# A graph layer on one core: layer 0's keys by nodes, its norms a round further ahead, two steps on GpSimd, six zero scatters, and the last group's transposes inside the context

## Chip, core, metric

One core of one Trainium2 chip runs the whole kernel. The metric is the device time of one execution in microseconds (us), as a median over runs. The engines are written as in the profile: PE (TensorE matmul), PEld (its weight loads), DVE (VectorE), ACT (ScalarE), POOL (GpSimd), SP (SyncE, which only issues DMAs here).

## What is computed

The reference takes 6250 nodes of 256 features and 106250 edges of 64 features:

```python
xn = _layernorm(x)
x = x + gnn(xn, edges, u) + mix(xn)          # mix: four layers, below
x = x + ffn(_layernorm(x))                   # one of 32 experts for each node

# one layer of mix
h = _layernorm(x, ln1_g[i], ln1_b[i])
q = softmax(split(h @ Wq) * scale, axis=-1)  # over the 32 features of a head
k = softmax(split(h @ Wk) * scale, axis=-2)  # over all 6250 nodes
v = split(h @ Wv)
context = einsum('bhnd,bhne->bhde', k, v)
x = x + einsum('bhnd,bhde->bhne', q, context) @ Wo + bo
x = x + gelu(layernorm2(x) @ W1 + b1) @ W2 + b2
```

The gnn term sums the edges' features by source node. The softmax of `k` runs over the nodes, so its maximum and sum go over all groups of nodes before the context is complete.

## The kernel before

The nodes lie in 13 groups: twelve of 4 tiles of 128 nodes, and a last one (g = 12, `NG - 1`) of 106 nodes. `X` keeps all nodes in SBUF. Every engine runs its instructions in the order in which the code issues them; that order is written out by hand, and buffers come from pools that are used in turn. PSUM has six banks for matmuls (`mm`) and two for the edges' sums (`seg`). A float32 matmul leaves two records in the trace, so 8 matmuls in the code are `x16` in the views.

The part that the change is about mostly is layer 0's first half: it makes q, k and the context for all groups, before the first feed-forward block (`ff_in`, L258). Its loop runs over g = 0 to 11. A round g of the loop is, in the code before:

- `keys_t(g-1)` (L685, copies L687): transposes the exponentials of k of the group before, which lie by features (128 features by 512 nodes), to nodes by features, 8 transposes;
- `norms_b(g+1)` (L346 to L359): reciprocals and products for the double norm (the input's norm and the layer's own), the scaling of `X` (L353, four on DVE), ACT's square root (L351) and ACT's scaled copy to `z` (L359);
- `norms_a(g+2)` (L337, L338, L339): mean and variance of the tiles on DVE, square root on ACT;
- `keys(0, g, then=rest)`: k by features, 4 matmuls of 128x512 (L534), the maximum over the nodes (L535), the running maximum and ACT's exponential from PSUM with its sum (L554); between them `rest`, that is `queries_t(g-1)` (L698, copies L701) and `queries` twice (matmuls L575, maximum L584, difference L585, exponential L587);
- `queries_norm` twice (sum L594, reciprocal L595, product L596, all on DVE);
- `context(g-1)`: 8 matmuls (L715) and the running update (L721);
- `norm1_t(0, g+1)`: 8 transposes of `z` (L148) and ACT's scaled copies to `hT` (L152).

Rounds 1, 3, 5 and 7 also carry a little work for the edges on DVE: casts of the source numbers (L384, L808), and `edge_match` and `edge_split` (L431, L448, L450).

Layers 1 to 3 make their keys in another way, by nodes: `keys_n` (8 matmuls L609, two copies to SBUF L612, two maxima L616 and L617), `keys_max` (2 transposes L625, reduction L627), `keys_less` (2 transposes L645, two differences L648), `keys_exp` (exponentials in SBUF) and `context_n` (8 matmuls L667 of 257 columns, where a column of ones makes the sum of k). The feed-forward matmuls fill most of those layers. At the end of each of them the last full group and the group of 106 nodes take the old way, with `keys`, `context` and `norm1_t`.

The edges go through POOL: 831 scatters (L483) that add rows to four tables in HBM. Each waits until the scatter four before it has landed. Near the end POOL also scatters the nodes to the experts' table `xtab` (L1104) and the results to the output (L1201). Until its first edge scatter POOL has only memsets, iotas and one select to do.

Of the kernel before, what the change touches and what calls it, by code (L numbers as in the profile page):

```python
# [63 lines left out]
def graph_layer_kernel(ctx, tc, x, src, srct, edge, cols, rows, rwt, gw1, gw2, wq, wk, wv, wo, w1, w2, xw, out):  # L64
# [41 lines left out]
    def group(g):  # L106

        i0 = 4 * g
        n = min(4, NT - i0)
        r = min(P, N - i0 * P)  # L110
        return i0, n, r, i0 * P, min(512, N - i0 * P)
# [49 lines left out]
    with ExitStack() as body:  # L161
# [124 lines left out]
        with ExitStack() as mix:  # L286
# [44 lines left out]
            def norms_a(g):  # L331
                i0, n, r, t0, cnt = group(g)
                st = small.tile([P, 4, 6], F32, name="st")
                mv = small.tile([P, 4, 2], F32, name="mv")
                sd = small.tile([P, 4], F32, name="sd")
                for j in range(n):
                    nc.vector.bn_stats(out=st[:r, j, :], in_=X[:r, i0 + j, :])  # L337
                    nc.vector.bn_aggr(out=mv[:r, j, :], in_=st[:r, j, :])  # L338
                nc.scalar.activation(sd[:r, :n], mv[:r, :n, 1], AF.Sqrt, bias=eps[:r], scale=1.0)  # L339
                LN[g] = mv, sd  # L340

            def norms_b(g):
                i0, n, r, t0, cnt = group(g)
                mv, sd = LN.pop(g)
                rs = small.tile([P, 4], F32, name="rs")
                nc.vector.reciprocal(rs[:r, :n], sd[:r, :n])  # L346

                v1 = small.tile([P, 4], F32, name="v1")
                nc.vector.tensor_tensor(out=v1[:r, :n], in0=mv[:r, :n, 1], in1=rs[:r, :n], op=ALU.mult)
                nc.vector.tensor_tensor(out=v1[:r, :n], in0=v1[:r, :n], in1=rs[:r, :n], op=ALU.mult)  # L350
                nc.scalar.activation(v1[:r, :n], v1[:r, :n], AF.Sqrt, bias=eps[:r], scale=1.0)  # L351
                for j in range(n):
                    nc.vector.tensor_scalar(out=X[:r, i0 + j, :], in0=X[:r, i0 + j, :], scalar1=mv[:r, j, 0:1],  # L353
                                            scalar2=rs[:r, j:j + 1], op0=ALU.subtract, op1=ALU.mult)
                rs1 = small.tile([P, 4], F32, name="rs1")
                nc.vector.reciprocal(rs1[:r, :n], v1[:r, :n])
                Z1[g] = z = z1(g)
                for j in range(n):
                    nc.scalar.activation(z[:r, j, :], X[:r, i0 + j, :], AF.Copy, scale=rs1[:r, j:j + 1])  # L359


            per_row = ep.tile([P, 5], F32, name="per_row", bufs=1)
            expo, wgt, twice, dump = (per_row[:, i:i + 1] for i in range(4))
            nc.gpsimd.iota(expo, pattern=[[0, 1]], base=63, channel_multiplier=-1, allow_small_or_imprecise_dtypes=True)
            nc.scalar.activation(wgt, expo, AF.Exp, scale=float(np.log(3.0)))
# [6 lines left out]
            half = qT[:, 1, N - 2 * ET:N - ET].bitcast(I16)[:, :ET]  # L372
            nc.sync.dma_start(out=wide, in_=srct.rearrange("o (p t) -> (o p) t", p=P))
            near_row = near.rearrange("(o p) t -> o (p t)", o=1)
            dumpi = per_row[:, 4:].bitcast(I32)
            nc.gpsimd.iota(dumpi, pattern=[[0, 1]], base=TDUMP, channel_multiplier=1)
            ebuf = [ep.tile([P, CB * EB, DE + 2], F32, name=f"edge{i}", bufs=1) for i in range(4)]
            for t in ebuf:
# [13 lines left out]
            def clear_tabs():  # L392
                for t in tabs:
                    tv = t.rearrange("(q p r) c -> q p (r c)", q=TQ, p=P)
                    for q in range(TQ):
                        nc.sync.dma_start(out=tv[q], in_=zero)

            def clear(e):
                nc.sync.dma_start(out=xtab[e * XCAP:e * XCAP + XCLEAR, :].rearrange("(p r) c -> p r c", p=P),
                                  in_=zero[:, :XROW].unsqueeze(1).to_broadcast([P, XCLEAR // P, XROW]))  # L400

            EDGE, ALL, EQ, SUM, PART = {}, {}, {}, {}, {}
            steps = {"load": 0, "match": 0, "split": 0, "sum": 0, "add": 0}
# [115 lines left out]
            def norm1_t(l, g):  # L519
                i0, n, r, t0, cnt = group(g)  # L520

                HT1[g] = ap.tile([P, 2, 512], F32, name="hT1") if g + 1 < NG else ffp.tile([P, 2, 512], F32, name="hT2")
                transposed(HT1[g], [Z1[g][:, j, :] for j in range(n)], n, r, cnt, C_G1 + 2 * l, C_B1 + 2 * l)
# [63 lines left out]
                nc.scalar.activation(q[:r, :mh], q[:r, :mh], AF.Exp, scale=QK_SCALE)  # L587
                QS[g, which] = q, mh

            def queries_norm(g, which):  # L590
                q, mh = QS[g, which]
                r = group(g)[2]
                sm = small.tile([P, 2 * HEADS], F32, name="sm")
                nc.vector.tensor_reduce(out=sm[:r, :mh], in_=q[:r, :mh], axis=AX.X, op=ALU.add)  # L594
                nc.vector.reciprocal(sm[:r, :mh], sm[:r, :mh])  # L595
                nc.vector.tensor_tensor(out=q[:r, :mh], in0=q[:r, :mh],  # L596
                                        in1=sm[:r, :mh].unsqueeze(2).to_broadcast([r, mh, DH]), op=ALU.mult)


            def keys_n(l, g):  # L600
                h, w = HT1[g], WQ[l]
                kn = []
                both = [bank(), bank()]

                for j in range(2):
                    for k in range(2):
                        for i, ps in enumerate(both):
                            c = (2 * i + j) * P
                            nc.tensor.matmul(ps[:, j * D:(j + 1) * D], h[:, k, c:c + P], w[:, k, D:2 * D], start=(k == 0), stop=(k == 1))  # L609
                for ps in both:  # L610
                    t = ap.tile([P, 512], F32, name="ek", bufs=2)
                    nc.scalar.copy(t, ps)  # L612
                    kn.append(t)

                top = ap.tile([P, 512], F32, name="kt", bufs=2)
                nc.vector.tensor_tensor(out=top, in0=kn[0], in1=kn[1], op=ALU.max)  # L616
                nc.vector.tensor_tensor(out=top[:, :D], in0=top[:, :D], in1=top[:, D:], op=ALU.max)  # L617
                KN[g] = kn, top
# [85 lines left out]
                keys_t(g)  # L704
                queries_t(g)

            def context(g, blocks=(0, 1)):

                i0, n, r, t0, cnt = group(g)
                kt, alpha = KT[g]  # L710
                z = Z1[g]
                ps = bank().rearrange("p (b c) -> p b c", b=2)
                for b in blocks:
                    for j in range(n):
                        nc.tensor.matmul(ps[:, b, :], kt[b][:r, j * P:(j + 1) * P], z[:r, j, :], start=(j == 0), stop=(j == n - 1))  # L715
                if g == 0:
                    ctxt["C"] = ap.tile([P, 2, D], F32, name="C")
                    nc.vector.tensor_copy(ctxt["C"], ps)
                else:
                    for b in blocks:  # L720
                        nc.vector.scalar_tensor_tensor(out=ctxt["C"][:, b], in0=ctxt["C"][:, b], scalar=alpha[:, b:b + 1],  # L721
                                                       in1=ps[:, b], op0=ALU.mult, op1=ALU.add)
# [50 lines left out]


            norms_a(0)
            norms_b(0)
            norm1_t(0, 0)
            norms_a(1)
            norms_a(2)
            norms_b(1)  # L780
            clear_tabs()
            load_wo(0)
            load_bo(0)
# [2 lines left out]
            for g in range(NG - 1):  # L786
                if g == 0:
                    keep_warm(6)
                elif g > 1:
                    keys_t(g - 1)  # L790
                if g:
                    norms_b(g + 1)
                if g and g + 2 < NG:
                    norms_a(g + 2)

                def rest():
                    if g:
                        queries_t(g - 1)
                    queries(0, g, 0)
                    queries(0, g, 1)  # L800

                keys(0, g, then=rest)
                for i in range(2):
                    queries_norm(g, i)
                if g:
                    context(g - 1)
                if g == 3:
                    nc.vector.tensor_copy(half, wide)  # L808
                    nc.sync.dma_start(out=near, in_=half)
                    edge_load()  # L810
                    edge_load()
                elif g == 5:
                    edge_match()
                    edge_split()
                    edge_load()
                elif g == 7:
                    edge_match()
                    edge_split()
                norm1_t(0, g + 1)
                if g == 0:  # L820
                    keys_t(0)
                elif g == 1:
                    edge_tables()
            keys_t(NG - 2)

            def last_steps(l):

# [1 line left out]
                queries_t(g, (0,), between=lambda: keys_t(g + 1))  # L829
                context_last(l, (lambda: (queries_norm(g + 1, 0), queries_t(g, (1,))), lambda: queries_t(g + 1)))  # L830

            keys(0, NG - 1, then=lambda: queries(0, NG - 1, 0))
            context(NG - 2)
            last_steps(0)


            for l in range(DEPTH - 1):
# [66 lines left out]
                norm1(g + 1)  # L904
                queries_norm(g, 1)
                context(g, (0,))
                norm1_t(n, g + 1)
                context(g, (1,))
                keys(n, g + 1, then=lambda: queries(n, g + 1, 0))
                if n + 1 == DEPTH:  # L910
                    while steps["add"] < NEB:
# [607 lines left out]
```

## Time and profile before

| | |
|---|---|
| median of 3 runs | 2731.92 us (2731.6 to 2733.16) |
| the profiled execution | 2705.55 us, its span 2703.8 us |
| TensorE clock granted | 0.997 |
| PE busy | 2663.4 us, 99% |
| DVE busy | 1751.4 us, 65% |
| ACT busy | 1146.2 us, 42% |
| POOL busy | 1475.7 us, 55% |
| layer 0's first half | from the start to 193.3 us, where the first L258 begins |
| POOL's first edge scatter | 201.56 us |

The profiled execution was 26.4 us shorter than the median of the runs. A span starts at the first instruction and ends at the last. Line numbers are those of the kernel before; in the changed kernel the same code stands some lines further down. The views give the start of a group of instructions, its length, and in brackets the idle time of its engine just before it with what ended it.

### The profile page before, as it was taken

What the parts mean: (1) busy time and instruction counts of PE and PEld (TensorE: products, weight loads), DVE (VectorE), ACT (ScalarE), POOL (GpSimd) and SP (SyncE); (2) the same over time, 40 slices, a digit from 0 to 9 for tenths busy, and PEclk for the clock granted to TensorE, in tenths of its full rate; (3) what the DMA queues carried; (4) which work ended last, traced back from release to release, by engine and by line L of the source; (5) the groups of instructions that cost most, each with busy time, mean ns of one, the idle gap of its engine ahead of it and who ended that gap; (6) DMA issues with size and microseconds to landing.
All of it is one profiled execution on the core that took longest, in us unless ns stands there. A gap on an engine that the chain in (4) does not pass through costs nothing.

```text
span 2703.8 us, 38523 instructions
## 1 busy us (share of the span) xinstructions
PE 2663.4 (99%) x13639; PEld 1954.9 (72%) x13639; DVE 1751.4 (65%) x4692; ACT 1146.2 (42%) x1999; POOL 1475.7 (55%) x1117
## 2 busy tenths in 40 slices
PE   9999999999999999999999999999999999999997
PEld 6777777777777777777767777777776676677675
DVE  8976766767568667676677766666645455454474
ACT  7764443534445444343544444435422322332333
POOL 0006777777777787887867878778300100100166
PEclk9999999999999999999999999999999999999998
DMA  8006555555665556555645555544411111111362
GB/s 261 16 11 90 64 80 65 83 63 68 85 100 70 78 61 85 64 74 73 97 75 80 65 81 65 66 48 46 92 24 32 32 32 32 32 27 31 111 226 77
DMA packets 371471, 193.58 MB, mean 72 GB/s; under 512 B 265770, under 2 KB 363790, under 8 KB 371272
## 3 DMA queue, kind: packets, MB, share of 16 engines
q1 hardware_dynamic: 245416, 150.44, 22.8%
q0 software_dynamic: 125856, 40.61, 20.3%
q8 instruction: 110, 1.80, 0.3%
q14 instruction: 89, 0.73, 0.1%
HBM read 108.78 MB, written 85.70 MB: 72 GB/s over the span
## 4 chain that ended last, share of the span: by engine, by line
PE 89%; DVE 3%; ACT 2%; DMA 2%; POOL 2%; SPq 1%; issue 1%; POOLq 0%; ACTq 0%; DVEq 0%
PE mm L258 25%; PE mm L278 25%; PE mm L197 6%; PE mm L575 5%; PE mm L609 5%; PE mm L667 4%; PE mm L1006 3%; PE mm L148 3%; PE mm L1047 3%; POOL out_x L1201 1%; PE mm L715 1%; PE mm L698 1%; ACT hT L152 1%; DMA tab<-zero 1%; PE mm L1011 1%; PE mm L534 1%
## 5 line engine op out<-in xcount | busy, mean ns | idle before, releaser
L483 POOL DMA_INDIRECT tab<-s,row x831 | 1335.9, 1608 | 584.1 <-issue 227.2
L258 PE MATMUL mm<-hT,w 128*128 128x512 f32 (+1 forms) x1664 | 705.9, 572 | 0.6 <-ACT hT L152 0.4
L278 PE MATMUL mm<-w,hid 128*128 128x256 f32 x3120 | 690.6, 380 | 0.0
L278 PEld LDWEIGHTS mm<-w,hid 128*128 128x128 f32 x3120 | 587.7, 190 | 78.7
L258 PEld LDWEIGHTS mm<-hT,w 128*128 128x128 f32 x1664 | 294.7, 190 | 298.1 <-issue 285.0
L262 ACT ACTIVATE hid<-mm,col 128x512 f32<-128x512 f32 (+1 forms) x416 | 266.1, 662 | 288.0 <-PE mm L258 287.3
L1104 POOL DMA_INDIRECT xtab<-rows,to x49 | 48.1, 983 | 572.6 <-DVE to L1102 473.0
L134 ACT ACTIVATE sd<-mv,eps 128x2 f32<-128x2 f32 (+2 forms) x161 | 47.6, 296 | 692.5 <-DVE mv L133 692.3
L280 DVE TENSOR_TENSOR X<-mm,X 128x512 f32<-128x512 f32 (+1 forms) x99 | 67.6, 683 | 284.0 <-PE mm L278 284.0
L152 ACT ACTIVATE hT<-mm,col 128x512 f32<-128x512 f32 (+1 forms) x208 | 145.2, 751 | 95.4 <-PE mm L148 95.4
L575 PE MATMUL mm<-wqkv,hT 128*128 128x256 f32 (+1 forms) x784 | 177.7, 379 | 0.0
L197 PE MATMUL mm<-M,qT 128*128 128x256 f32 x720 | 163.4, 379 | 0.0
L135 DVE RECIPROCAL rs<-sd 128x2 f32<-128x2 f32 (+2 forms) x161 | 27.4, 170 | 209.3 <-ACT sd L134 209.3
L575 PEld LDWEIGHTS mm<-wqkv,hT 128*128 128x128 f32 (+1 forms) x784 | 147.3, 190 | 19.9 <-issue 0.5
L197 PEld LDWEIGHTS mm<-M,qT 128*128 128x128 f32 x720 | 133.4, 190 | 16.6
L431 DVE TENSOR_TENSOR eq<-all,srcf 128x512 bf16<-128x512 int16 x208 | 142.5, 685 | 0.1
L199 DVE TENSOR_TENSOR X<-mm,X 128x512 f32<-128x512 f32 (+1 forms) x92 | 62.2, 676 | 119.2 <-PE mm L197 119.2
L132 DVE BATCH_NORM_STATS2 st<-X 128x6 f32<-128x256 f32 (+1 forms) x327 | 132.6, 406 | 2.7
L609 PE MATMUL mm<-wqkv,hT 128*128 128x256 f32 x528 | 122.8, 386 | 2.3
L140 DVE TENSOR_SCALAR z<-X,mv,rs 128x256 f32<-128x256 f32 (+1 forms) x327 | 121.6, 424 | 4.8
L148 PE MATMUL mm<-ident,z 128*128 128x128 f32 x882 | 118.8, 274 | 3.7 <-DVE z L140 2.8
L667 PE MATMUL mm<-z,ek 128*128 128x257 f32 x528 | 120.2, 380 | 0.0
(288 smaller groups left out, 4021.4 us busy)
## 6 DMA issues: line engine op xcount, KB each, us to landing
xtab<-zero SPq DMA_DIRECT2D x32, 1036.0 KB
edge<-in_edge SPq DMA_DIRECT2D x207, 128.0 KB
all<-near SPq DMA_DIRECT2D x207, 128.0 KB
tab<-s,row POOLq DMA_INDIRECT x831
w<-in_w SPq DMA_DIRECT2D x8, 1024.0 KB
xg<-xtab SPq DMA_DIRECT2D x26, 259.0 KB
tab<-zero SPq DMA_DIRECT2D x40, 162.5 KB
tb<-tab SPq DMA_DIRECT2D x48, 130.0 KB
```

What stands on the lines that cost most here:

```text
L132: nc.vector.bn_stats(out=st[:r, j, :], in_=source(j))
L148: nc.tensor.transpose(ps[:, j * P:j * P + r], z[j][:r, k * P:(k + 1) * P], ident[:r, :r])
L152: nc.scalar.activation(hT[:, k, :cnt], ps[:, :cnt], AF.Identity, bias=col[:, bcol + k:bcol + k + 1], scale=col[:, gcol + k:gcol + k + 1])
L197: nc.tensor.matmul(ps[:r, j, :], qT[:, k, c0:c0 + r], M[:, k, :], start=(k == 0), stop=(k == 1))
L258: nc.tensor.matmul(part[i], w[:, k, b * P:(b + 1) * P], h[:, k, :cnt], start=(k == 0), stop=(k == 1))
L262: nc.scalar.activation(hid[:, :cnt], part[i], AF.Gelu, bias=col[:, c:c + 1], scale=1.0)
L278: nc.tensor.matmul(ps[:r, j, :], hid[b][:, c0:c0 + r], w[:, b, :], start=(b == 0), stop=(b == NHB - 1))
L431: nc.vector.tensor_tensor(out=eq[:, :m], in0=ALL.pop(b)[:, :m], in1=srcf[:, t0:t0 + m].unsqueeze(2).to_broadcast([P, m, P]), op=ALU.is_equal)
L483: nc.gpsimd.indirect_dma_start(out=tabs[i], out_offset=bass.IndirectOffsetOnAxis(ap=row[:, i:i + 1], axis=0), in_=s[:, i, :DE + 1], in_off ...
L575: nc.tensor.matmul(ps[:r, j * D:(j + 1) * D], h[:, k, (j0 + j) * P:(j0 + j) * P + r], w[:, k, :D], start=(k == 0), stop=(k == 1))
L609: nc.tensor.matmul(ps[:, j * D:(j + 1) * D], h[:, k, c:c + P], w[:, k, D:2 * D], start=(k == 0), stop=(k == 1))
L667: nc.tensor.matmul(ps[:, :D + 1], kn[j // 2][:, c:c + P], z[:, j, :], start=(j == 0), stop=(j == 3))
```

## The change

In layer 0's first half the keys of groups 0 to 11 are made by nodes, as in the later layers. The norms are split into five steps (`norms_a`, `norms_a_root`, `norms_b`, `norms_b_root`, `norms_z`) and run a round earlier: `norms_a` for g+3, `norms_b` for g+2, `norms_z` for g+1. The square roots of a round stand side by side on ACT. From g = 2 on, the scaling of `X` is POOL's; so is the last product of `queries_norm` in this loop. `norm1_t(g+1)` moves up to stand before `keys_less`. Six indirect scatters of zeros to unused rows of `xtab` come before the first edge scatter; they write the same rows, and each waits for the one before it. The copies of k take buffers of `hid`. In layers 1 to 3, the last group's transposes move from before the second block of `context(g, (1,))` into its middle.

```diff
+            def norms_a_root(g):
+                i0, n, r, t0, cnt = group(g)
+                mv = LN[g]
+                sd = small.tile([P, 4], F32, name="sd")
                 nc.scalar.activation(sd[:r, :n], mv[:r, :n, 1], AF.Sqrt, bias=eps[:r], scale=1.0)
                 LN[g] = mv, sd
...
-                v1 = small.tile([P, 4], F32, name="v1")
+                LN[g] = v1 = small.tile([P, 4], F32, name="v1")
                 nc.vector.tensor_tensor(out=v1[:r, :n], in0=mv[:r, :n, 1], in1=rs[:r, :n], op=ALU.mult)
                 nc.vector.tensor_tensor(out=v1[:r, :n], in0=v1[:r, :n], in1=rs[:r, :n], op=ALU.mult)
+
+                scale = nc.vector if g < 2 else nc.gpsimd
+                for j in range(n):
+                    scale.tensor_scalar(out=X[:r, i0 + j, :], in0=X[:r, i0 + j, :], scalar1=mv[:r, j, 0:1],
+                                        scalar2=rs[:r, j:j + 1], op0=ALU.subtract, op1=ALU.mult)
+
+            def norms_b_root(g):
+                i0, n, r, t0, cnt = group(g)
+                v1 = LN[g]
                 nc.scalar.activation(v1[:r, :n], v1[:r, :n], AF.Sqrt, bias=eps[:r], scale=1.0)
-                for j in range(n):
-                    nc.vector.tensor_scalar(out=X[:r, i0 + j, :], in0=X[:r, i0 + j, :], scalar1=mv[:r, j, 0:1],
-                                            scalar2=rs[:r, j:j + 1], op0=ALU.subtract, op1=ALU.mult)
+
+            def norms_z(g):
+                i0, n, r, t0, cnt = group(g)
+                v1 = LN.pop(g)
                 rs1 = small.tile([P, 4], F32, name="rs1")
                 nc.vector.reciprocal(rs1[:r, :n], v1[:r, :n])
                 Z1[g] = z = z1(g)
...
+            nowhere = per_row[:, 5:].bitcast(I32)
+            nc.gpsimd.iota(nowhere, pattern=[[0, 1]], base=NX * XCAP, channel_multiplier=1)
+
+            def even_out():
+
+                for _ in range(6):
+                    nc.gpsimd.indirect_dma_start(out=xtab, out_offset=bass.IndirectOffsetOnAxis(ap=nowhere, axis=0),
+                                                 in_=zero[:, :XROW], in_offset=None)
...
-            def queries_norm(g, which):
+            def queries_norm(g, which, by=nc.vector):
...
-                nc.vector.tensor_tensor(out=q[:r, :mh], in0=q[:r, :mh],
+                by.tensor_tensor(out=q[:r, :mh], in0=q[:r, :mh],
                                         in1=sm[:r, :mh].unsqueeze(2).to_broadcast([r, mh, DH]), op=ALU.mult)
...
-                    t = ap.tile([P, 512], F32, name="ek", bufs=2)
+
+                    t = ap.tile([P, 512], F32, name="ek", bufs=2) if l else ffp.tile([P, 512], F32, name="hid", bufs=NHB)
                     nc.scalar.copy(t, ps)
...
-            def context(g, blocks=(0, 1)):
+            def context(g, blocks=(0, 1), between=None):
...
                     for j in range(n):
+                        if between is not None and 2 * j == n:
+                            between()
                         nc.tensor.matmul(ps[:, b, :], kt[b][:r, j * P:(j + 1) * P], z[:r, j, :], start=(j == 0), stop=(j == n - 1))
...
             norms_a(0)
+            norms_a_root(0)
             norms_b(0)
+            norms_b_root(0)
+            norms_z(0)
             norm1_t(0, 0)
             norms_a(1)
+            norms_a_root(1)
             norms_a(2)
+            norms_a_root(2)
             norms_b(1)
+            norms_b_root(1)
+            norms_b(2)
+            norms_z(1)
+            norms_b_root(2)
             clear_tabs()
...
             for g in range(NG - 1):
                 if g == 0:
                     keep_warm(6)
-                elif g > 1:
-                    keys_t(g - 1)
+                else:
+                    keys_exp(g - 1)
+                    norms_z(g + 1)
+                    if g + 2 < NG:
+                        norms_b(g + 2)
+                if g + 3 < NG:
+                    norms_a(g + 3)
+                keys_n(0, g)
                 if g:
-                    norms_b(g + 1)
-                if g and g + 2 < NG:
-                    norms_a(g + 2)
-
-                def rest():
-                    if g:
-                        queries_t(g - 1)
-                    queries(0, g, 0)
-                    queries(0, g, 1)
-
-                keys(0, g, then=rest)
+                    queries_t(g - 1)
+                    if g + 2 < NG:
+                        norms_b_root(g + 2)
+                if g + 3 < NG:
+                    norms_a_root(g + 3)
+                queries(0, g, 0)
+                keys_max(g)
+                queries(0, g, 1)
+                norm1_t(0, g + 1)
+                keys_less(g)
+                if g:
+                    context_n(g - 1)
                 for i in range(2):
-                    queries_norm(g, i)
-                if g:
-                    context(g - 1)
+                    queries_norm(g, i, by=nc.gpsimd)
...
-                norm1_t(0, g + 1)
-                if g == 0:
-                    keys_t(0)
-                elif g == 1:
+                if g == 1:
                     edge_tables()
-            keys_t(NG - 2)
+            keys_exp(NG - 2)
+            even_out()
...
-            keys(0, NG - 1, then=lambda: queries(0, NG - 1, 0))
-            context(NG - 2)
+            keys(0, NG - 1, then=lambda: (queries(0, NG - 1, 0), context_n(NG - 2)))
             last_steps(0)
...
-                norm1_t(n, g + 1)
-                context(g, (1,))
+                context(g, (1,), between=lambda: norm1_t(n, g + 1))
```

More of the change, by code (lines that the diff above doesn't have):

```diff
@@ L334, in norms_a @@
                 mv = small.tile([P, 4, 2], F32, name="mv")
-                sd = small.tile([P, 4], F32, name="sd")
                 for j in range(n):
@@ L338, in norms_a @@
                     nc.vector.bn_aggr(out=mv[:r, j, :], in_=st[:r, j, :])
+                LN[g] = mv
+            def norms_a_root(g):
+                i0, n, r, t0, cnt = group(g)
+                mv = LN[g]
+                sd = small.tile([P, 4], F32, name="sd")
                 nc.scalar.activation(sd[:r, :n], mv[:r, :n, 1], AF.Sqrt, bias=eps[:r], scale=1.0)
@@ L359, in norms_b @@
                     nc.scalar.activation(z[:r, j, :], X[:r, i0 + j, :], AF.Copy, scale=rs1[:r, j:j + 1])
-            per_row = ep.tile([P, 5], F32, name="per_row", bufs=1)
+            per_row = ep.tile([P, 6], F32, name="per_row", bufs=1)
             expo, wgt, twice, dump = (per_row[:, i:i + 1] for i in range(4))
@@ L374, in graph_layer_kernel @@
             near_row = near.rearrange("(o p) t -> o (p t)", o=1)
-            dumpi = per_row[:, 4:].bitcast(I32)
+            dumpi = per_row[:, 4:5].bitcast(I32)
             nc.gpsimd.iota(dumpi, pattern=[[0, 1]], base=TDUMP, channel_multiplier=1)
```

## The prediction

> **What bounds the kernel now.** I read the page's engine totals first, then the stretches of layer 0's first half, then the chain of waits through them.
>
> ```profile
> span 2703.8 us, 38523 instructions
> PE 2663.4 (99%) x13639; PEld 1954.9 (72%) x13639; DVE 1751.4 (65%) x4692; ACT 1146.2 (42%) x1999; POOL 1475.7 (55%) x1117
> POOL 0006777777777787887867878778300100100166
> ```
>
> PE is busy for 99% of the span, so a gain must come from fewer PE instructions or from PE's 40 us of idle time. POOL's first slices are empty: there the change puts its new POOL work. Next come five rounds of the loop, the busy columns being PE, PEld, DVE, ACT, POOL:
>
> ```profile
> 45.50:59.17 13.67, 13.21 (x64) 10.02 (x65) 12.17 (x36) 10.81 (x23) 0.00 (x0) 1.00 0.90 247
> 86.54:100.70 14.16, 13.21 (x64) 10.03 (x65) 13.45 (x39) 10.82 (x23) 0.00 (x0) 1.00 0.07 19
> 142.23:155.32 13.09, 13.09 (x64) 10.04 (x65) 10.65 (x29) 10.63 (x22) 0.00 (x0) 1.00 0.00 0
> ```
>
> A plain round takes 13.68, PE idling 0.47; a round with edge work (g = 5 and 7) takes 14.16 with 0.95 idle; the last rounds, with fewer norms, are PE's own 13.09. All these rounds hold barely 7 us of idle PE. The chain says who holds PE up:
>
> ```profile
> 104.40 0.87 PE mm L148 x8
> 105.27 0.89 PE mm L685 x8
> ...
> 106.27 0.66 ACT kt L687 x2
> 106.93 0.43 issue
> 107.36 1.28 ACT L351
> ...
> 111.28 1.18 DVE gm L535 x2
> ```
>
> From the context the chain goes through the transposes and copies of k, ACT's load of the root's table, `norms_b`, `norms_a`, the two maxima and a round's softmax steps back to the next context. The change breaks exactly this chain. All edge work after layer 0's first half lies in PE-bound layers, so a shift of this half's end carries to the end of the run.
>
> **PE's work in a round.** Before: L534 3.44, L575 3.46, L715 3.5, and L698, L148, L685 0.87 each: 13.0 to 13.1. After: L609 3.46, L575 3.46, L667 3.48, L698 and L148 0.87 each, `keys_max` and `keys_less` 0.22 each: 12.58. PE loses 0.51 a round.
>
> **The new chain of a round.** Its pieces have rows in layers 1 to 3:
>
> ```profile
> 278.70 1.07 ACT L612 COPY ek<-mm 128x512 f32<-128x512 f32 x2 [2.50 <-PE mm L609]
> 279.80 0.69 DVE L616 TENSOR_TENSOR kt<-ek 128x512 f32<-128x512 f32 x1 [3.40 <-ACT ek L612]
> 280.53 0.43 DVE L617 TENSOR_TENSOR kt<-kt 128x256 f32<-128x256 f32 x1
> ```
>
> Count from the end of a context. DVE updates C (0.46), makes the sums and reciprocals of both queries (1.80), then the reciprocal for z (0.20): 2.46. ACT scales z (1.71) and copies k (1.07): 5.24. The two maxima take 1.16: 6.4. PE has by then done `keys_n`, `queries_t` and the first queries, 3.46 + 0.87 + 1.73 = 6.06, and waits 0.3 to 0.4 for `keys_max`. Then follow `keys_max` 0.3, second queries 1.73, `norm1_t` 0.87, `keys_less` 0.22, context 3.46 and hand-overs 0.26: 13.2 to 13.3. A plain round gains 0.45, not PE's whole 0.51 + 0.47.
>
> In the edge rounds eq (0.60), rest (0.35) and low (0.42), 1.37 in all, stand between the queries' sums and the reciprocal for z, so they enter the chain whole: 14.6, a loss of 0.45.
>
> **The sum with engines that don't disturb each other.** Start: ACT ends z of group 1 at 17.04, as before, then makes the extra root and copies k (0.30 + 1.07), where it went on to the exponentials; maxima 1.16, two pairs of maximum and difference for the queries (2 × 1.41), `keys_less`, the exponentials and hT (0.42 + 0.63 + 0.75) bring the second group's keys to 24.2 to 24.9, where they began at 22.84. I take +2.2. Nine rounds from the first context (31.82) to the tenth (155.32), 123.5 before: four plain ones at -0.45, two edge rounds at +0.45, the first +0.3 (DVE is still late from the start), the one with the long cast +0.06, and the last, PE-bound before and chain-bound now, +0.1: -0.45. After that PE bounds: one round's 0.51 and one dropped L685 of 0.87, -1.4. The layer ends: the moved transposes remove this wait, three times,
>
> ```profile
> 758.05 0.37 PE L148 MATMUL mm<-ident,z 106*128 106x106 f32 x2 [0.53 <-DVE z L140]
> ```
>
> 3 × 0.53 = -1.6; the block's first two matmuls (4 records, 0.86) cover z now, and hT's copy, 0.77, lies beside its last two (0.86); without that cover the 0.53 stays. In all +2.2 - 0.45 - 1.4 - 1.6 = -1.25.
>
> **The two steps on POOL.** No row shows a POOL product or scaling. The nearest:
>
> ```profile
> L381 POOL MEMSET zero<- 128x325 f32 x1 | 0.4, 361 | 0.0
> masks.py:199 POOL TENSOR_SCALAR_AFFINE_SELECT ident<-ident 128x128 f32<-128x128 f32 x1 | 0.3, 291 | 0.1
> ```
>
> The memset of 4 columns takes 0.094, so writing costs 0.83 ns a column: 0.52 for the product's 512, 0.31 for the scaling's 256. The select reads and writes one operand, 1.6 ns a column: 0.91 and 0.50. A second operand could double that: 1.7 and 0.9. I take 1.1 for the product (two inputs, a little above the select's rate) and 0.5 for the scaling (one input, the select's rate). At 1.1 POOL's two products end at 1.36 + 2.2 = 3.56 after the context, 0.1 after `keys_n` (3.46), hidden by the wait for `keys_max`. X of group g+2 is needed a round later, so the scalings (4 × 0.5) are hidden; were they later than that, the next round's z would be too, one for one. Taking the products from DVE (2 × 0.69) is already in the chain above.
>
> **Contention.** The trace of before never has a POOL operation on SBUF beside DVE in these rounds, so what they cost each other is bounded by nothing and by full turns: a DVE operation with two SBUF inputs waits until POOL's current one ends. With full turns, `norms_b`'s products (0.17 each; no chain by themselves) come up at 2.56 while the second product runs to 3.56: 1.0 late. DVE then needs 0.3 and four pairs for `norms_a` (2.12), ending at 6.0 where k's copies end at 5.24: +0.8 in each of seven rounds, 5.5. In edge rounds eq comes up at 2.26 and waits 1.3 for both products, and rest, low or a maximum some 0.7 for a scaling: 2 × 2.0. Start +0.8, for the first scalings against the maxima. Together 5.6 + 4 + 0.8 = +10.4, at the price taken. Between nothing and full turns I take full turns, since most of POOL's new 4.2 us a round falls on a DVE that is busy for 12 of 13.7, and give the low end its own case.
>
> The Trainium skill, "SBUF — State Buffer", section "Who interferes with whom", speaks against this change: a DVE instruction with two SBUF inputs and a GpSimd instruction that reads SBUF exclude each other for the whole of the instruction that began first. By it the sum is the one with full turns; no row here shows it yet. The skill's "GPSIMD Engine Reference", section 3.1, has 4.5 us for a two-input operation of 2048 columns against DVE's 2.3; an estimate from it for 512 is 1.12 us, and the rule there is to leave elementwise work to DVE.
>
> **Edits at nothing.** The six scatters of zeros, each waiting for the landing before it (up to 5 us with the issue of 0.97, by the scatters of L1201 and L1104), fit into POOL's idle time between its last product, near 170, and 201.56; they cost up to 5 if they spill over, but tables lag PE there. Behind them on POOL stand only the edge scatters, and SP's zeros to the same table, needed hundreds of us later. The end of the run, POOL's own scatters, is not touched. The square roots side by side keep two table loads of 1.28 a round, and the queries' exponentials that stand behind them are not what the new chain waits for: 6.4 passes before the loads, and ACT is busy for 10.8 of 13.7. New waits on DVE, the maxima for k's copies, have the query steps queued behind them; those are in the chain above. Copies of k in `hid`'s buffers: free until the first feed-forward.
>
> **The rivals.** (a) Contention as above: -1.25 + 10.4 = +9, or 3 to 16 by POOL's price and the share of turns: the low end is turns at the write rates (0.52, 0.31), where both products are done by 2.4 and nothing of `norms_b` is late, the high end a product at 1.4, 0.6 later in each of nine rounds, and rest and low each late for a scaling. (b) No contention: -1.25, within 3, which is how well the start and the hand-overs are known. (c) Faster: `keys_max` doesn't wait, so rounds fall to PE's 12.58. Nine of them take 113.2 against 123.5 now: with start, last rounds and layer ends -10.3 + 2.2 - 1.4 - 1.6 = -11. This decides if the chain above is 0.4 shorter than the rows say. Against it: its rows are measured in the same kernel; for it: the last rounds before reach PE's bound. (d) Slower still: POOL's operations cost 1.7 and 0.9. Its products end at 4.8, `norms_b` waits 2.2 and the round grows by 2.0, so 9 × 2.0 and edge rounds and start on top: +20 to +33. It decides from a product above 1.35, where even without turns `queries_t` holds PE. For it: GpSimd's select rate is that of one operand; against it: the write rate is half of it. That the change doesn't do what it says has one form: that keys by nodes still wait in ACT's line behind the roots' table load; the copies stand before the roots in the issue order, so no.
>
> **How the numbers follow.** The profiled run was 2705.55, 26.4 below the median 2731.92; I add the shift to the median: 2731.92 + 9 = 2741. Chances: (a) 0.48, (b) 0.24, (c) 0.15, (d) 0.13. 0.2%, 5.5 us, is about what a measurement of this kernel can tell from no change. (a) gives 0.36 slower and 0.12 same; (b) 0.22 same, 0.02 faster; (c) 0.15 faster; (d) slower. The range reaches from (c), -11, to the lower part of (d), +22: 2721 to 2754; (a) alone would be 2735 to 2748.
>
> **What would show it.** Right: POOL products near 1.1; DVE's `norms_b` products beginning when a POOL operation ends; contexts 14.0 apart in plain rounds, 16 to 17 in edge rounds; the first feed-forward near 204 (193.34 + 2.2 - 0.45 - 1.4 + 10.4); no PE wait before the three moved transposes. Case (b): contexts 13.2 apart. Case (c): 12.6, no PE wait before `keys_max`. Wrong altogether: a first edge scatter over 15 us later than 201.56, or a shift after 200 us that the first half doesn't show.

## The result, and the profile after

| | before | after | ratio (95% interval) |
|---|---|---|---|
| median of 19 runs each | 2732.08 us | 2736.56 us | 1.0015 (1.0008 to 1.0021) |
| again, in the session of the experiments (15 and 11 runs) | 2705.76 us | 2709.63 us | 1.0017 (1.0008 to 1.0026) |

The change makes the kernel about 4 us slower, some 0.15%; the forecast was 9 us, in a range from 11 faster to 22 slower. The two rows come from two sessions. The second session used three chips, each with its own runs of the kernel before (2708.0 in one run, 2707.04 and 2705.76 as medians), and totals are compared only on one chip. In the first session's profile of the changed kernel the scatters of the results, near the end, stop ten times for 2 to 6 us; in the profiles of the second session, and in the first profile of before (2705.55), they stop at most once, for up to 2 us. So the 26.4 us between that profile and the median of the runs shown with it look like a difference between sessions and not like a fixed offset; adding the shift to the median did no harm. What makes the stops was not settled. The account below sets the changed kernel (`e9_after`, span 2708.5) against the kernel before (`e4_before`, span 2705.55), both of the second session but of two chips; their first halves agree with the first profiles within 0.2 us.

The page of the changed kernel (first session), busy times and POOL by slices:

```profile
span 2731.3 us, 38722 instructions
PE 2668.2 (98%) x13687; PEld 1971.2 (72%) x13687; DVE 1749.6 (64%) x4653; ACT 1138.8 (42%) x1973; POOL 1562.0 (57%) x1189
POOL 4536887877777777877767878778201001001166
```

POOL has work from the first slice on. Two stretches of its layer 0, from one context to the next, a plain round and an edge round (busy columns PE, PEld, DVE, ACT, POOL):

```profile
78.72:92.77 14.05, 12.99 (x70) 11.06 (x69) 12.04 (x32) 10.41 (x19) 7.08 (x6) 1.00 0.00 1
92.77:108.80 16.03, 12.99 (x71) 11.06 (x70) 13.65 (x35) 10.22 (x19) 7.56 (x6) 1.00 0.07 16
```

PE has less to do, as forecast, and yet a plain round is 0.37 longer than before and an edge round 1.87. The time goes where PE waits for the second maximum, for 0.92 in the plain round and 2.45 in the edge round (L650 is `keys_max`, L723 is `queries_t`):

```profile
89.70 0.41 PE L650 MATMUL mm<-ident,kt 128*128 128x128 f32 x2 [0.92 <-DVE kt L642]
```

```profile
100.67 0.87 PE L723 MATMUL mm<-ident,q 128*128 128x128 f32 x6 [0.59 <-POOL q L620]
105.73 0.41 PE L650 MATMUL mm<-ident,kt 128*128 128x128 f32 x2 [2.45 <-DVE kt L642]
```

DVE is as busy in these rounds as before (12.04 against 12.17 in a plain one); with POOL's work left out it is busy for 10.91 (`e2_nopool`, below). The timeline of the plain round, DVE first, then POOL, says why. Before, the second product of `norms_b` took 0.16:

```profile
L350 DVE TENSOR_TENSOR v<-v,rs 128x4 f32<-128x4 f32 x5 | 0.8, 163 | 0.2
```

Now it is L355:

```profile
84.86 0.28 DVE L354 TENSOR_TENSOR v<-mv,rs 128x4 f32<-128x4 f32 x1
85.17 0.97 DVE L355 TENSOR_TENSOR v<-v,rs 128x4 f32<-128x4 f32 x1
...
88.89 0.67 DVE L642 TENSOR_TENSOR kt<-kt 128x256 f32<-128x256 f32 x1
```

```profile
84.07 2.06 POOL L620 TENSOR_TENSOR q<-q,sm 128x512 f32<-128x512 f32 x2 [6.96 <-DVE sm L619]
86.11 5.05 POOL L359 TENSOR_SCALAR X<-X,mv,rs 128x256 f32<-128x256 f32 x4
```

L355 multiplies four columns. It takes 0.97 and ends at 86.14, when POOL's second product ends at 86.13. The wait for POOL doesn't stand in the brackets as idle time: it is inside the DVE operation's own length. The second maximum, L642, takes 0.67 instead of 0.43 beside the scalings.

At the layer ends the wait of 0.53 before the transposes is gone; L148 follows the context's matmuls directly:

```profile
764.56 2.76 PE L742 MATMUL mm<-z,kt 128*128 128x256 f32 x12
767.16 0.35 PE L148 MATMUL mm<-ident,z 106*128 106x106 f32 x2
767.34 0.83 PE L742 MATMUL mm<-z,kt 128*128 128x256 f32 x3
```

By parts, in the second session (us):

| part | before | after | measured | forecast |
|---|---|---|---|---|
| to the first context | 31.87 | 34.60 | +2.73 | +3.0 |
| nine rounds, first to tenth context | 123.51 | 130.67 | +7.16 | +9.15 |
| to the first feed-forward | 38.03 | 36.83 | -1.20 | -1.4 |
| to the last feed-forward (three layer ends) | 2366.14 | 2363.96 | -2.18 | -1.6 |
| from there to the end | 146.00 | 142.44 | -3.56 | 0 |
| span | 2705.55 | 2708.50 | +2.95 | +9.15 |

The part before the span, called the tail below, is the least certain: in the four profiles of kernels without the six scatters it took 144.3 to 146.0, in the second session's seven with six 141.0 to 142.4.

### The profile page after: what moved, and what is told of

Its sections match the earlier page's. It is cut to its first block, busy times and chain, and to the rows that moved or that the text cites. A ratio compares the mean times of both kernels' runs of the same rounds, so it can differ in the third digit from the quotient of the medians.

```text
span 2731.3 us, 38722 instructions
## 1 busy us (share of the span) xinstructions
PE 2668.2 (98%) x13687; PEld 1971.2 (72%) x13687; DVE 1749.6 (64%) x4653; ACT 1138.8 (42%) x1973; POOL 1562.0 (57%) x1189
## 5 line engine op out<-in xcount | busy, mean ns | idle before, releaser
L633 PE MATMUL mm<-wqkv,hT 128*128 128x256 f32 x720 | 166.3, 384 | 4.0 <-ACT hT L152 1.7
L633 PEld LDWEIGHTS mm<-wqkv,hT 128*128 128x128 f32 x720 | 133.9, 190 | 25.3 <-ACT hT L152 7.0
L148 PE MATMUL mm<-ident,z 128*128 128x128 f32 x882 | 118.7, 274 | 2.1 <-DVE z L140 1.2
```

The costliest lines, as they stand in the source:

```text
L148: nc.tensor.transpose(ps[:, j * P:j * P + r], z[j][:r, k * P:(k + 1) * P], ident[:r, :r])
```

## The experiments

All labels are runs of the second session. "Rounds" are the distances of contexts in the profile. e1 to e4, e11 and e12 are single runs, read by their profiles.

**e1_noprod: without POOL's products.**

```diff
-                by.tensor_tensor(out=q[:r, :mh], in0=q[:r, :mh],
+                if by is nc.vector:
+                    by.tensor_tensor(out=q[:r, :mh], in0=q[:r, :mh],
                                         in1=sm[:r, :mh].unsqueeze(2).to_broadcast([r, mh, DH]), op=ALU.mult)
```

> Leaves out POOL's products of the loop (q stays unnormalised there); POOL's scalings of X stay. In the changed kernel plain rounds are 14.04 apart, edge rounds 16.03, and the second product of norms_b takes 0.97 where the first takes 0.28. Theory (DVE's operations with two SBUF inputs wait for POOL's current one): without the products that one takes 0.16 again, plain rounds 13.2 to 13.4 apart, edge rounds 14.6 to 15, first feed-forward near 197. Rival (the new chain is as long by itself, POOL costs it nothing): plain rounds stay at 14.0, edge rounds at 16.0, first feed-forward near 202.

Measured: plain rounds 13.38, edge rounds 14.77, first feed-forward 195.78. Two groups of DVE over six rounds:

```profile
L643 DVE TENSOR_TENSOR kt<-kt 128x256 f32<-128x256 f32 x6 | 2.5, 425 | 0.2
L355 DVE TENSOR_TENSOR v<-v,rs 128x4 f32<-128x4 f32 x6 | 1.0, 162 | 0.2
```

L355 is back at 0.16. The products cost 14.04 - 13.38 = 0.66 in a plain round and 16.03 - 14.77 = 1.26 in an edge round. The transposes that read them wait on PE, 0.14 in a plain round and 0.59 in an edge round of the changed kernel, but PE stands still for longer behind that, waiting for the maximum, so this wait is hidden.

This run shows something else: the scalings read SBUF too, and L355 runs beside one of them. A plain round, DVE, then POOL's four scalings, then the third of them alone:

```profile
82.77 0.16 DVE L355 TENSOR_TENSOR v<-v,rs 128x4 f32<-128x4 f32 x1
85.33 0.81 DVE L642 TENSOR_TENSOR kt<-hid 128x512 f32<-128x512 f32 x1 [0.20 <-ACT hid L638]
```

```profile
82.64 5.06 POOL L359 TENSOR_SCALAR X<-X,mv,rs 128x256 f32<-128x256 f32 x4 [8.33 <-DVE rs L351]
```

```profile
85.06 1.21 POOL L359 TENSOR_SCALAR X<-X,mv,rs 128x256 f32<-128x256 f32 x1
```

L355 ends at 82.93, while the first scaling lasts until 83.87. The first maximum, L642, begins 0.28 after the third scaling and ends at 86.14, before that scaling's end at 86.27; it takes 0.81 instead of 0.69. The theory as written, a wait for POOL's current operation whatever it is, would have had both wait for a scaling's end. In the changed kernel (30 to 200 us) it is the same: of 23 DVE operations with two SBUF inputs that begin during a scaling, 15 end before it; of 17 that begin during a product, none does.

**e2_nopool: without products and without POOL's scalings of X.**

```diff
-                    scale.tensor_scalar(out=X[:r, i0 + j, :], in0=X[:r, i0 + j, :], scalar1=mv[:r, j, 0:1],
+                    if g < 2:
+                        scale.tensor_scalar(out=X[:r, i0 + j, :], in0=X[:r, i0 + j, :], scalar1=mv[:r, j, 0:1],
...
```

The edit of e1 is in it too.

> Leaves out the products of the loop and POOL's scalings of X too (groups 2 to 12 stay unscaled). Theory of turns: the sum without contention, plain rounds 13.2, edge rounds 14.6, the second maximum of keys_n back at 0.43 where it takes 0.67, first feed-forward near 194 to 195. Rival (chain as long by itself): 14.0 and 16.0, near 202.

The stretches of a plain and an edge round:

```profile
75.35:88.52 13.17, 12.76 (x70) 11.07 (x69) 10.91 (x32) 10.40 (x20) 0.00 (x0) 1.00 0.01 1
88.52:103.08 14.56, 12.77 (x71) 11.08 (x69) 12.27 (x35) 10.41 (x20) 0.00 (x0) 1.00 0.11 19
```

First feed-forward 193.59, where it was 193.41 before. That is the prediction's sum without contention, 13.2 and 14.6, piece by piece: the new chain is not longer than its rows, and the whole loss of the first half, 202.10 - 193.59 = 8.5, is what POOL costs. The second maximum is back at 0.42.

**e3_memset: POOL as busy, but not reading SBUF.**

```diff
-                by.tensor_tensor(out=q[:r, :mh], in0=q[:r, :mh],
+                if by is nc.vector:
+                    by.tensor_tensor(out=q[:r, :mh], in0=q[:r, :mh],
                                         in1=sm[:r, :mh].unsqueeze(2).to_broadcast([r, mh, DH]), op=ALU.mult)
+                else:
+                    for _ in range(2):
+                        by.memset(q[:r, :mh], 1.0 / DH)
```

> Each product is replaced by two POOL memsets of the same q (about 1.04 us together, no reading of SBUF; q becomes a constant). Theory that POOL's reading excludes DVE's second input: rounds as without products, 13.2 to 13.4 and 14.6 to 15. Rival within it (any POOL operation on SBUF excludes DVE, or POOL being busy delays something): 14.0 and 16.0 as with products.

Rounds 13.59 and 14.76. The same two products of `norms_b`, and POOL beside them:

```profile
83.93 0.16 DVE L354 TENSOR_TENSOR v<-mv,rs 128x4 f32<-128x4 f32 x1
84.13 0.16 DVE L355 TENSOR_TENSOR v<-v,rs 128x4 f32<-128x4 f32 x1
...
87.42 0.75 DVE L646 TENSOR_TENSOR kt<-kt 128x256 f32<-128x256 f32 x1
```

```profile
82.80 2.15 POOL L625 MEMSET q<- 128x512 f32 x4 [6.62 <-DVE sm L618]
84.94 4.82 POOL L359 TENSOR_SCALAR X<-X,mv,rs 128x256 f32<-128x256 f32 x4
```

The memsets run at 83.93 to 84.29 too, and L354 and L355 don't notice them: an operation of POOL that only writes doesn't hold DVE's second input. That any reading does is not shown: the products, which hold it for their whole length, read two tensors, and the scalings, which read one and two scalars for each partition, let L355 pass in e1. The plain round misses the expected 13.2 to 13.4 by 0.2. With the memsets in front the scalings come later, and the two maxima, which meet them elsewhere, take 1.44 together in a plain round instead of e1's 1.23. The first feed-forward, 197.88, is 2.1 later than e1's; about 1.1 of this lies before the first context, where this profile has a stretch of lower clock (granted 0.72 on the mean from 20 to 26).

**e5_fast: the same work, DVE in another order.** Nothing goes back to DVE; what it did after the context is issued before it. For this `norms_z` keeps only the reciprocal, and `norms_b` only the reciprocal and products; the copies to `z` and POOL's scalings become steps of their own, which stay in the next round. The edit where the order changes:

```diff
                 keys_less(g)
+                if g + 2 < NG:
+                    norms_z(g + 2)
+                if g + 3 < NG:
+                    norms_b(g + 3)
+                for i in range(2):
+                    queries_norm(g, i, by=nc.gpsimd)
                 if g:
                     context_n(g - 1)
-                for i in range(2):
-                    queries_norm(g, i, by=nc.gpsimd)
```

> The changed kernel, with DVE's order in layer 0's loop rearranged and nothing left out: the reciprocal for z (norms_z's first line, group g+2), norms_b's reciprocal and products (group g+3) and both queries' sums come before context_n(g-1) instead of after it, so they run in DVE's wait for that context, before POOL's products start. Theory (the chain is context's end, sums, reciprocal for z, z, copies of k, maxima, plus the turns): both are off the chain, z starts at the context's end, and PE sets the round: 12.6 to 12.8 apart in plain rounds, 12.6 to 14.0 in edge rounds, first feed-forward at 186 to 189, the whole 8 to 13 us faster than before on the same chip. Rival (something else of the round, such as ACT's table loads or the later release of the context's banks, comes right behind): plain rounds 13.2 to 13.6, first feed-forward 192 to 196, the whole within 6 us of before.

A plain and an edge round:

```profile
74.50:87.08 12.58, 12.58 (x70) 11.16 (x69) 11.17 (x32) 10.43 (x19) 6.99 (x6) 1.00 0.01 1
87.08:100.58 13.50, 12.77 (x71) 11.08 (x69) 12.59 (x35) 10.43 (x19) 7.82 (x6) 1.00 0.12 21
```

Plain rounds are PE's own 12.58, busy for all of it. The median is 2694.97 against 2707.04 for before, ratio 0.9958 (0.9944 to 0.9972). Of these 12 us some 5.5 are the layer ends and the six scatters, which the changed kernel has too; the order itself is the 16 between that kernel, 3.9 slower than before, and this one. First feed-forward 188.28, of which about 1.5 us is a stretch of lower clock (granted 0.72 on the mean from 20 to 26) that the profile of e10, with the same order up to there, doesn't have.

**e6_between: the kernel before with the moved transposes alone.**

```diff
-                norm1_t(n, g + 1)
-                context(g, (1,))
+                context(g, (1,), between=lambda: norm1_t(n, g + 1))
```

> The kernel before with only the layer ends of the change (the last group's transposes between the two halves of the context's second block). Expected: first feed-forward at 193.4 as before, the last layer's feed-forward 2.2 earlier (0.73 for each of three layers, as in the changed kernel; the prediction had 0.53), the whole 1.6 to 2.3 faster, if nothing behind gives it back; rival: the end is set by POOL's scatters of the results at a rate of their own, then too it moves with the feed-forward's end, so only a longer tail (from the last feed-forward's begin to the end: 146.0) would speak against it.

The last feed-forward begins at 2557.55 after a first one at 193.52, that is 2364.03 against 2366.14, -2.1. The part behind it took 144.6, not longer. Median 2704.89 against 2707.04, ratio 0.9991 (0.9982 to 1.0).

**e7_even and e8_noeven: the six scatters alone, and the change without them.**

```diff
             keys_t(NG - 2)
+            even_out()
```

> The kernel before with only the six scatters of zeros added. On this chip the tail (from the last feed-forward's begin to the end of the span) took 146.0 in the kernel before and 141.1 to 141.7 in the three variants of the changed kernel. If the six scatters make the difference (they move which of POOL's DMA semaphores each later scatter takes), this kernel has a tail of 141 to 142 and is 4 to 5 us faster; if they do nothing, as the prediction said, 146 and no change within 2.

```diff
             keys_exp(NG - 2)
-            even_out()
```

> The changed kernel without the six scatters. Expected if they shorten the tail: tail 146, whole 4 to 5 us slower than the changed kernel, so 10 to 12 us slower than before on the same chip (first half 8.9, layer ends -2.2). If they do nothing: tail 141 to 142, whole 2 to 3 slower than before. First feed-forward at 202.3 in both cases.

e7: 2703.61 against 2707.04, ratio 0.9987 (0.9978 to 0.9996), tail 142.1. e8: 2714.33 against 2707.04, ratio 1.0031 (1.0021 to 1.0041), tail 144.3. The six scatters are worth 3.4 us, in both kernels: e7 gains that, and e8 is 7.3 slower than before on its chip, the changed kernel 3.9 on its own. The expected 4 to 5 came from the 146.0 of one profile of before, the longest of four. The expected 10 to 12 for e8 doesn't follow from its own parts: 8.9 - 2.2, with the tail as before, is 6.7, near what was measured. e8's first feed-forward, 204.0, is 1.7 late; its profile has a stretch of lower clock (granted 0.76 from 45 to 52). The results' scatters themselves get no faster with the six: they stand 1.29 apart instead of 1.277, 1 us in all. The gain lies after the last one, in steps of POOL's queue that close the execution. The `DRAIN` there, of e4_before and of e7 (shortest/median/longest of three, ns):

```profile
L1515 POOLq DRAIN  x3: 46/107/8031, 2696.7 to 2705.3; - x3
```

```profile
L1525 POOLq DRAIN  x3: 46/107/4356, 2698.2 to 2703.1; - x3
```

8.03 us become 4.36, and the step ahead of it (`INC_SWDGE_SEM`) falls from 2.14 to 1.23, together 4.6. In e8, without the six, both are back at 8.03 and 2.14.

**e12_even3 and e11_even12: other numbers of such scatters.** The line of e7 with 3 and with 12 in place of 6.

> The kernel before with three scatters of zeros. If the closing cost falls with each scatter added: INC_SWDGE_SEM 1.7 and DRAIN 6.2. If it goes by steps: the values of none (2.14, 8.03) or of six (1.23, 4.36).

> The kernel before with twelve scatters of zeros instead of none or six. At the end POOL's last two steps after the last scatter, INC_SWDGE_SEM and DRAIN, took 2.14 and 8.03 without extra scatters and 1.23 and 4.36 with six. If the cost falls with each scatter added (0.15 and 0.61 each), twelve give 0.3 and 0.7; if it is a matter of steps or of a remainder, it is one of the two values known or another.

`DRAIN` took 4.19 with three and 4.93 with twelve, in one profile each; both kernels ran 2703.41, 2.35 less than before on their chip. So it doesn't fall with each one; it rises slowly, and somewhere between none and three it drops. A remainder of the number of all scatters might do that, but no run shows it, and the cause of the drop stays open.

**e4_before and e9_after: both kernels beside the experiments.**

> The kernel before once more, for a second profile of its last 150 us. In the profile of before the scatters of the results follow one another every 1.28 us without a break and the span is 2703.8, while all timed runs are near 2732; in the changed kernel's profile they stop some ten times for 2 to 6 us. If these stops belong to the kernel whatever the change, they are in this profile too, the span is near 2730 and the first feed-forward still at 193.3. If they come with the change, the span is near 2704 again.

> The changed kernel itself, on the chip of these experiments. From the parts: first half +8.9, three layer ends -2.2, six scatters -3.4 (e7), the sum +3.3 against before on the same chip, 0.12%; first feed-forward at 202.3, the span's end 9.2 after the last scatter, and the results' scatters without the long stops that the changed kernel's first profile shows. Rival (the stops belong to the change): span near 2731 again.

e4: span 2705.55, first feed-forward 193.41, one stop of 2 us. e9: 2709.63 against 2705.76, first feed-forward 202.10, one stop of 1.7; the sum of the parts was +3.3, the medians differ by 3.9.

**e10_best: e5_fast with the edges' work in four rounds.**

```diff
                 elif g == 5:
                     edge_match()
-                    edge_split()
                     edge_load()
                 elif g == 7:
                     edge_match()
+                elif g in (6, 8):
                     edge_split()
```

> The rearranged order of e5_fast, with edge_match and edge_split of groups 5 and 7 in successive rounds (5, 6, 7, 8) instead of in one. e5_fast's edge rounds are 13.5 apart, because eq, rest and low and a POOL scaling beside them make the maxima 0.73 late; half of that work fits in DVE's slack of a round. Expected: all rounds of g = 5 to 8 at 12.6 to 12.9, first feed-forward 1.0 to 1.8 earlier than e5_fast's on equal clock (186 to 187.5), the whole 12 to 14 faster than before. Rival: the slack is not there, two rounds of 12.6 become 13.0 to 13.2 and nothing is gained.

The contexts of those rounds stand 12.79, 12.81, 12.62 and 12.57 apart; first feed-forward 185.36, 1.4 earlier than e5's if the 1.5 of its lower clock are taken off; the median 2692.32 against 2705.76, ratio 0.9949 (0.9935 to 0.9962). It is the fastest of all, 13 us ahead of before.

```profile
72.94:85.51 12.57, 12.57 (x70) 11.15 (x69) 11.16 (x32) 10.43 (x19) 6.99 (x6) 1.00 0.01 1
85.51:98.30 12.79, 12.77 (x70) 11.08 (x69) 11.96 (x33) 10.43 (x19) 7.61 (x6) 1.00 0.08 21
```

## Why the prediction was right, and where its terms were off

**The mechanism.** Rival (a) it was, for POOL's products: turns between them and DVE's operations with two SBUF inputs. The forecast that `norms_b`'s products would come up while the second product runs and wait for its end is L355 at 85.17 (L354, before it, meets the end of the first). The wait then shows as PE's wait for the maximum, 0.92 where e2, without POOL's work, has 0.41. Rival (b) is what e2 measures, 193.59; rival (d) fell with the product's price. That the measured time lies in the range says little by itself, as the range took in nearly every case named.

**Full turns failed for the scalings.** The sum had rest, low or a maximum wait some 0.7 for one. But a DVE operation with two inputs runs inside a scaling (L355 in e1, with its usual 0.16) or is slowed by 0.1 to 0.3; in the edge rounds rest and low met no scaling, and the first maximum lost 0.13 to one. The Trainium skill's rule in "SBUF — State Buffer", "Who interferes with whom", which spoke against the change, agrees with L355's 0.97 beside a product, and also in that an operation of GpSimd that only writes doesn't contend (0.16 beside e3's memsets). Beside the scalings, which read SBUF, the measurement differs from it and decides: the turn is not for the whole of the instruction. What part of a scaling holds DVE up stays open.

**A match that is in part luck.** Plain rounds were to be 14.0 apart and are 14.04. The sum's 0.8 for them came from `norms_b`'s products alone; by e1 and e2 POOL's products cost 0.66 and the scalings, at nothing in a plain round of the sum, 0.2.

**The product's price** was taken as 1.1 and is 1.05 undisturbed, 1.12 on the mean. The estimate of 1.12 from the skill's "GPSIMD Engine Reference", section 3.1, was as good.

**The scaling's price failed:** 0.5 taken, 0.31 to 0.9 as bounds, 1.22 measured, so neither the memset's nor the select's rate bounded an operation with two scalars for each partition. It cost little, 13.38 - 13.18 = 0.2 a round: the scalings lie behind the products in POOL's queue, they meet only the maxima, and they don't hold these for their whole length. By the sum's own rule of full turns, 1.22 would have put the forecast higher still: that two wrong terms met here is luck.

**The edge rounds** were priced at +2.0 each and took +1.47 (16.03 - 14.56). DVE gets its turn between the two products, too: eq takes 1.02 instead of 0.63 and rest 1.26 instead of 0.41, 1.24 together, and POOL's second product waits for eq (the pair takes 2.50 there, 2.06 in a plain round). The prediction had eq wait for both, and a scaling on top.

**The number of rounds** that pay 0.8 was seven in the sum and should have been fewer. The last two, with one tile of `norms_a` or none, have the slack to hide the wait: 13.36 and 13.21, 0.18 and 0.02 above e2's. The edge rounds' 2 × 0.53 and these 2 × 0.8 - 0.2 make 2.5; the other rounds paid a little more than 0.8 (1.06 in the first, 0.96 in the one with the long cast), which leaves 1.85 of the 2.0 by which the nine rounds were overpriced; the rest is the sum without contention, 0.1 too long.

**The layer ends** gave 0.73 each, not 0.53. The view's wait counts from the end of the last matmul, and a matmul is shown for 0.38 while in a row they start every 0.22. The lost time between starts was 0.91 - 0.22 = 0.69.

**"The end of the run is not touched" failed.** The six scatters hid in POOL's idle time, as said, but shorten the closing `DRAIN`. I had taken what follows the last scatter for a constant. The step stands in the trace of before as well, 8.03 us long, behind the last scatter. This term and the overpriced rounds put the result at half the forecast.

**Rival (c)** was given 0.15 on the condition that the chain to `keys_max` be 0.4 shorter. It isn't in this kernel; e5 made it so by taking the reciprocal for z and the sums out of the chain, and got rival (c)'s 12.58.

The scalings alone back on DVE, with the products left on POOL, were not tried, so what the products cost without scalings behind them is known only as a difference.

## What to carry to other kernels

A two-input operation moved to POOL costs DVE nothing only where DVE has no two-input operation to issue meanwhile; look for short DVE operations whose own length has grown, for the wait isn't shown as idle time. What such a move needs is an order in which DVE's two-input work is issued before POOL starts, in DVE's wait for PE: the same instructions in another order went from 4 us slower than the kernel before to 12 us faster. When DMAs are added, look at what closes the execution too.

## What the runs showed of the hardware

- A two-input operation on POOL, 128x512 float32, took 1.05 us; a scaling by two scalars of each partition, 128x256, took 1.22, more than the product of twice the columns, and 0.41 on DVE. A memset of 128x512 took 0.54.
- DVE's operations with two SBUF inputs and POOL's products wait for each other inside the operation's length, both ways, one operation at a time (DVE 0.16 to 0.97; POOL's pair 2.06 to 2.50).
- With POOL's scalings they overlap: L355 took 0.16 inside one, the maxima 0.1 to 0.3 more than alone; a scaling beside such operations took up to 1.44 in e1 and 1.91 in e5, instead of 1.22.
- The closing `DRAIN` of POOL's queue took 8.03 us with no extra scatter, 4.19 with three, 4.36 with six, 4.93 with twelve.
- In one session the same two kernels ran 26 to 27 us longer than in the other. The one profile from there has its stops in the last 150 us; what causes them stays open.
